# Softmax denominators added up by GpSimd's accumulating transfers instead of VectorE, in an attention and local-attention kernel on one core

## The chip, the cores and the metric

The kernel runs on one core of a Trainium2 chip, in one launch. The metric is the device time of that launch in microseconds (us), the median of several runs. TensorE (PE), VectorE (DVE), ScalarE (ACT), GpSimd (POOL) and the queue of SyncE (SP) run side by side. Each executes its own instructions in the order in which the program gives them, and they wait for one another by semaphores.

## The reference, cut to what matters

`x` is 4 images of 64 x 64 pixels with 256 channels, in float32. Layer 0 is full self-attention over the 4096 pixels of an image; layer 1 is a depthwise 3x3 convolution, two 1x1 convolutions with a GELU between them, and a 3x3 windowed attention. Only layer 0's softmax is touched here.

```python
q = x @ Wq + bq                      # (4, 4096, 32)
k = x @ Wk + bk                      # (4, 4096, 32)
v = x @ Wv + bv                      # (4, 4096, 256)
attn = softmax(einsum('bnd,bmd->bnm', q, k), axis=-1)
x = gamma * einsum('bnm,bmc->bnc', attn, v) + x
# layer 1
h_new = x + up2(gelu(up1(depthwise3x3(x))))
out = h_new + local_attention_3x3(h_new)
```

The softmax is computed as `exp(energy)`, its product with `v`, and a division by the sum of the exponentials, the denominator. This document is about how the denominator is summed.

## The kernel before

The 4 x 4096 queries are cut into 32 slots of 512 queries, 8 slots to an image. A slot goes over the image's 4096 keys in 8 groups `G` of 512 keys, and each group in two halves of 256 keys. So a slot has 16 points, one for each half group; here p(n) with n = 2G + half is the tile of exponentials of point n, 128 x 1024 values (512 KB). The loop `for point in range(points)` writes the order of all the work by hand; no scheduler moves anything. At each point it emits, in this order:

- at the first half of a group: the loads for groups further on (`load_keys`, tile `ka`, `load_values`, tile `v`, both on SP's queue), and `energy`, four matmuls (L333) into the single PSUM tile `e`, one group ahead of the products;
- `weight`, the exponential of one half of `e` into `p` (L341, ACT), two points ahead of the products. The tag `p` has 3 buffers, so p(n+3) overwrites p(n);
- the point's `jobs`: layer 1 of the slots 2 to 5 blocks back (convolution on VectorE, `hidden_part`, `update_part`, `guide_part`, `scores`, `local_product`, `border` and so on). At point 12 stands `local_sum`, a chain on GpSimd of a memset, six additions (L1012) and one or two more (L1015) into `lsum`. At point 14 stands `border`, which ends in one or two small GpSimd operations on `pad` (L910, L914);
- `product(slot, G, half)`, the matmuls of p(n) with `v` into the two banks `acc` (L352);
- `add_up` of p(n+1) into the denominator tile `den`, on VectorE: a copy for p(0) (L363) and an addition for each of p(1) to p(15) (L366). The last call also folds `den` from 1024 to 512 columns (L368);
- steps of the convolution (L505, VectorE), by a fixed table `share`.

After the last point, `partial_sums` transposes `den` and, from slot 4 on, the `lsum` of a slot further back (L386), and reduces both into `parts` (L387). `finish(slot)` then puts a small matmul `dps` (L405) into TensorE's order, straight behind the last product and ahead of the next slot's first `energy`. VectorE takes its reciprocal (L408), spreads it (L394, L397), and scales `acc` into `o` (L417), which frees the `acc` banks for the next slot's first product.

At the start, `project_qk(0)` makes the first queries and keys, and 12 small transfers (L273) on SP's queue copy them into `qa_0` and `ka_0`, where the first `energy` reads them. `fetch(4)` and `fetch(5)` read the pixels of blocks 4 and 5 from HBM (L237), each block in two transfers of 256 KB, one for each half of the channels. GpSimd's queue loads layer 1's weights (`blqk`, `wperc`, `wup1`, `wup2` and others, L80) and computes mixed weights `wmix` from them (L551); they stand in slot 0 at point 8 of GpSimd's order, behind nothing but the setup.

From the second image on, `project_v` makes the values of the next image, through tiles `vs` (2 buffers), which ACT's queue stores to HBM (`packed_v`).

Of the kernel before, what the change touches and what calls it, by code (L numbers as in the profile page):

```python
# [12 lines left out]
ALU = mybir.AluOpType  # L13
# [3 lines left out]
P = 128  # L17
B, H, W, C = 4, 64, 64, 256
# [4 lines left out]
NB = 512  # L23
# [4 lines left out]
TPB = NB // P  # L28
# [25 lines left out]
def attention_then_perception_kernel(  # L54
# [19 lines left out]
    nc = tc.nc  # L74
# [17 lines left out]
    def unshifted():  # L92
# [6 lines left out]
        def tile_of(shape, tag, name, bufs=1):  # L99
            return pool.tile(shape, F32, tag=tag, name=name, bufs=bufs)  # L100
# [19 lines left out]
        def ring(slot):  # L120

            return 1 + slot % RING * RB
# [15 lines left out]
        for r in range(4):  # L138
            nc.scalar.dma_start(
                out=bqk2[r * CQK : (r + 1) * CQK, :], in_=b_qk[:, r % 2 : r % 2 + 1]  # L140
# [17 lines left out]
        for r in range(KR):  # L158
            m = near[r * KW : (r + 1) * KW]
            for half in range(2):  # L160

                for sign in (1, -1):
                    nc.gpsimd.affine_select(
                        out=m[:, half], in_=m[:, half], compare_op=ALU.is_ge, fill=0.0,
# [13 lines left out]
        for q in range(0, P, SQ):  # L178
            part = fold[q : q + SQ].rearrange("p (j r) -> p j r", r=SQ)
            nc.gpsimd.affine_select(  # L180
                out=part, in_=part, compare_op=ALU.not_equal, fill=1.0,
# [15 lines left out]
            return watched[:, i : i + 1]  # L197


        queries, keys, values, staged = {}, {}, {}, {}  # L200

# [10 lines left out]
        def fetch(s):  # L214

            b, g = divmod(s, NBLK)
            if 2 <= s < NBLK:

                if s == 2:
                    both = tile_of([P, NHC, NB], "hid", "xc_2_3")  # L220
                    staged[2], staged[3] = both[:, :CH], both[:, CH:]
                elif s == NBLK - 1:
                    t = tile_of([P, CH, UP + RB, W], "lq", f"xc_{s}")
                    staged[s] = t[:, :, UP:, :].rearrange("p c h w -> p c (h w)")
                elif s > 3:
                    t = tile_of([P, CH, 2, HALO + RB, KW], "h", f"xc_{s}", 3)
                    staged[s] = t.rearrange("p c a h w -> p (c a h w)")[:, : CH * NB].rearrange(
                        "p (c n) -> p c n", c=CH
                    )
            else:  # L230
                staged[s] = tile_of([P, CH, NB], "xc", f"xc_{s}", 2)
            rows = x[b].rearrange("p c (h w) -> p c h w", w=WP)
            at, of = (slice(r, r + RB) for r in (1 + g * RB, ring(s)))
            for c in range(CH):
                to = staged[s][:, c, :].rearrange("p (h w) -> p h w", w=W)
                if s >= RING:
                    nc.sync.dma_start(out=to, in_=rows[:, c, at, 1 : 1 + W])  # L237
                elif c == 0:
                    nc.vector.tensor_copy(to, xv[:, c, of, 1 : 1 + W])
                else:  # L240
                    nc.scalar.copy(to, xv[:, c, of, 1 : 1 + W])
# [50 lines left out]
        def project_v(s, pair, tag="m"):  # L292
            xc = staged[s]
            if s >= NBLK:
                v = tile_of([P, 2, C], "vs", f"vs_{s}_{pair}", 2)
            else:
                if pair == 0:
                    values[0, s] = tile_of([P, TPB, C], "v", f"v_0_{s}", 3)
                v = values[0, s][:, 2 * pair : 2 * pair + 2, :]
            ps = bank(tag, f"v_{s}_{pair}")  # L300
            for i in range(2):
                for kin in range(CH):
                    nc.tensor.matmul(  # L303
                        ps[:, i * C : (i + 1) * C],
                        lhsT=xc[:, kin, bass.ts(2 * pair + i, P)], rhs=wv[:, kin, :],
                        start=(kin == 0), stop=(kin == CH - 1),
                    )
            nc.scalar.copy(v, ps.rearrange("p (t c) -> p t c", c=C))
            nc.scalar.dma_start(
                out=packed_v[:, bass.ts(2 * s + pair, 2 * C)], in_=v.rearrange("p t c -> p (t c)")  # L310
            )
# [11 lines left out]
        energies, weights, sums, accs, lsums, lrdens = {}, {}, {}, {}, {}, {}  # L323
# [34 lines left out]
        def add_up(s, G, half):  # L358

            p = weights[s, G, half]  # L360
            if G == 0 and half == 0:
                sums[s] = tile_of([P, 2, NB], "den", f"den_{s}")
                nc.vector.tensor_copy(sums[s], p)  # L363
                return
            den = sums[s]
            nc.vector.tensor_tensor(den, den, p, ALU.add)  # L366
            if G == NG - 1 and half == 1:
                nc.vector.tensor_tensor(den[:, 0, :], den[:, 0, :], den[:, 1, :], ALU.add)  # L368

        def squares(t):  # L370
# [7 lines left out]
        def partial_sums(s):  # L378


            a = shared(s)
            parts_[s] = tile_of([P, 2, NJ], "parts", f"parts_{s}")
            turneds[s] = tile_of([P, CH, NB], "xc", f"turned_{s}", 2)
            todo = [sums[s][:, 0, :]] + ([] if a is None else [lsums.pop(a)])
            for i, t in enumerate(todo):
                nc.vector.transpose(turneds[s][:, i, :], t)  # L386
                nc.vector.tensor_reduce(  # L387
                    parts_[s][:, i, :], squares(turneds[s][:, i, :]), axis=AX.X, op=ALU.add
                )
            watch(parts_[s][:, : len(todo), :].rearrange("p i j -> p (i j)"))  # L390
# [8 lines left out]
        def finish(s, parts=((0, RB),)):  # L399

            acc = accs.pop(s)
            n = NJ * (1 if shared(s) is None else 2)
            ps = bank("m", f"dps_{s}")[:, :n]
            given = parts_.pop(s).rearrange("p i j -> p (i j)")[:, :n]
            nc.tensor.matmul(ps, lhsT=fold, rhs=given, start=True, stop=True)  # L405
            inverse = tile_of([P, 2, NJ], "inverse", f"inverse_{s}")
            inverses[s] = inverse
            nc.vector.reciprocal(inverse.rearrange("p i j -> p (i j)")[:, :n], ps)  # L408

            rden = sums.pop(s)[:, 1, :]  # L410
            on_all(inverse[:, 0, :], turneds[s][:, 0, :], rden)
            watch(inverse.rearrange("p i j -> p (i j)")[:, :n])
            os = [tile_of([P, NB], "o", f"o_{s}_{c}", 2) for c in range(CH)]
            for r0, r1 in parts:
                n = slice(r0 * W, r1 * W)
                for c, o in enumerate(os):
                    nc.vector.scalar_tensor_tensor(  # L417
                        o[:, n], acc[c][:, n], gam[:, 0:1], rden[:, n], ALU.mult, ALU.mult,
                        accum_out=seen(),
                    )  # L420
                for c, o in enumerate(os):
                    dst = xv[:, c, ring(s) + r0 : ring(s) + r1, 1 : 1 + W]
                    nc.vector.scalar_tensor_tensor(  # L423
                        dst, o[:, n].rearrange("p (h w) -> p h w", w=W), gbv[:, c : c + 1], dst,
                        ALU.add, ALU.add,
                    )
                if len(parts) > 1:
                    yield
            if s < NSLOT - 1:
                rim(s)  # L430
            yield
# [303 lines left out]
        guides, lvs, near_ws, late, results, totals = [], {}, {}, {}, {}, {}  # L735
# [183 lines left out]
        def local_values(s, t):  # L919
            ps = job_bank(f"lv_{s}_{t}")  # L920
            for half in range(2):
                for kin in range(CH):
                    nc.tensor.matmul(  # L923
                        ps[:, half * C : (half + 1) * C],
                        lhsT=keys_of(s, t, half, kin), rhs=wlv[:, kin, :],
                        start=(kin == 0), stop=(kin == CH - 1),
                    )
            for half in range(2):
                if s < NSLOT - 2:
                    lvs[s, t, half] = tile_of([P, C], "lv", f"lv_{s}_{t}_{half}", 8)  # L930
                else:
                    if not half:
                        late[s, t] = late_tile(f"lv_{s}_{t}")
                    lvs[s, t, half] = late[s, t][:, half * C : (half + 1) * C]
                lv = lvs[s, t, half]
                nc.vector.tensor_tensor(lv, ps[:, half * C : (half + 1) * C], blv, ALU.add)
                if s >= NSLOT - 1:

                    square = tile_of([P, 2, NB], "den", f"lv_{s}_{t}_{half}_2")[:, 0, :C]
                    nc.gpsimd.tensor_tensor(square, lv, lv, ALU.mult)  # L940
                    watch(square)

# [145 lines left out]

        fetch(0)
        fetch(1)  # L1090
        fetch(4)
        project_v(0, 0, "acc")
        project_qk(0)
        project_v(0, 1, "acc")
        fetch(2)
        fetch(3)
        fetch(5)
        for i in range(2):
            project_v(1, i)
# [21 lines left out]
        for slot in range(NSLOT):  # L1121
# [3 lines left out]
            k, a = slot - LAG_HID, slot - LAG_ATT  # L1125
# [50 lines left out]
            for point in range(points):  # L1176
                G, half = divmod(point, 2)
# [526 lines left out]
```

## Time and profile before

| what | before |
|---|---|
| median of 3 runs | 3395.23 us (3394.91 to 3396.22) |
| the profiled execution: its own time | 3395.35 us |
| its span, first to last instruction | 3393.6 us |
| PE busy | 3364.7 us (99%) |
| DVE busy | 2747.1 us (81%) |
| ACT busy | 1074.8 us (32%) |
| POOL busy | 352.1 us (10%) |
| granted TensorE clock, mean | 0.998 |
| GpSimd's own transfers (software_dynamic) | 576 packets, 2.53 MB |
| bytes moved by all transfers | 285.17 MB, mean 84 GB/s |

The span is 1.75 us shorter than the execution's own time. A busy PE is one with a matmul under way; matmuls are pipelined, and their ends are modelled. In the lists of groups, the numbers behind the bars are the total busy time and the mean duration in ns of one instruction, then the idle time of that engine just before the group and what ended most of it. In the lists of waits, the numbers are the total, how many times, and the longest. In the timeline, a row has the start, the duration, the engine, the line and operation, output and inputs, a count, and in brackets the idle time before it. In the list of transfers, the last number is the time in us from issue to landing, where the trace can tell it.

### The profile page before, as it was taken

How to read it: one execution, taken by the hardware profiler on the slowest of the kernel's cores; microseconds unless marked ns; L12 is line 12 of the kernel's file. 1: busy time of each engine (PE TensorE's matmuls, PEld its weight loads, DVE VectorE, ACT ScalarE, POOL GpSimd, SP SyncE). 2: the span in 40 equal slices, each digit the busy share in tenths (PEclk: the TensorE clock that was granted, in tenths of full speed). 3: DMA queues.
4: the chain of work that ended last, by engine and by line, in shares of the span. 5: the costliest groups of instructions: out<-in, count | busy, mean ns of one | idle time of the engine just before them, and what ended most of it. 6: DMA issues, size and time to landing. Idle time of an engine off the chain costs nothing.

```text
span 3393.6 us, 32830 instructions
## 1 busy us (share of the span) xinstructions
PE 3364.7 (99%) x11678; PEld 2118.8 (62%) x11678; DVE 2747.1 (81%) x4455; ACT 1074.8 (32%) x1344; POOL 352.1 (10%) x550
## 2 busy tenths in 40 slices
PE   8999999999999999999999999999999999999998
PEld 5556666666666666666666666666666666666655
DVE  2388888867888888876888888887688888988895
ACT  2233333333332333332333323333333333333331
POOL 3000011100111110110001111101110011110031
PEclk9999999999999999999999999999999999999999
DMA  5332222342222222234222222223422222222200
GB/s 170 104 104 65 73 77 78 97 133 89 77 77 81 82 75 71 77 102 140 77 78 78 75 82 83 67 79 107 141 80 68 78 77 70 87 84 66 71 13 26
DMA packets 166126, 285.17 MB, mean 84 GB/s; under 512 B 67284, under 2 KB 68196, under 8 KB 165828
## 3 DMA queue, kind: packets, MB, share of 16 engines
q1 hardware_dynamic: 155684, 263.36, 25.1%
q10 hardware_dynamic: 9696, 17.11, 1.3%
q0 software_dynamic: 576, 2.53, 0.2%
q8 instruction: 95, 1.56, 0.2%
q14 instruction: 75, 0.61, 0.1%
HBM read 240.23 MB, written 41.94 MB: 83 GB/s over the span
## 4 chain that ended last, share of the span: by engine, by line
PE 90%; DVE 7%; DMA 2%; SPq 0%; issue 0%; ACT 0%; ACTq 0%; DVEq 0%; POOL 0%
PE acc L352 47%; PE e L333 7%; PE hid_bc L610 5%; PE hid_de L610 4%; PE hid_gf L610 4%; PE lv L923 3%; DVE perc L505 3%; PE lo L1057 3%; PE v L303 2%; PE hid_a L610 2%; DMA ka<-packed 2%; PE s L964 2%; PE dx_cd L562 1%; PE dx_ab L562 1%; PE dx_eg L562 1%; DVE den L366 1%
## 5 line engine op out<-in xcount | busy, mean ns | idle before, releaser
L352 PE MATMUL acc<-p,v 128*128 128x512 f32 x4096 | 1833.3, 593 | 0.6 <-DVE o L417 0.6
L352 PEld LDWEIGHTS acc<-p,v 128*128 128x128 f32 x4096 | 770.4, 190 | 794.7 <-issue 775.4
L505 DVE SCALAR_TENSOR_TENSOR perc<-xp,wperc,perc 128x512 f32<-128x512 f32 (+2 forms) x1554 | 1108.1, 775 | 27.6 <-ACT perc L501 27.5
L341 ACT ACTIVATE p<-e 128x1024 f32<-128x1024 f32 x512 | 524.8, 1025 | 1676.9 <-PE e L333 758.3
L366 DVE TENSOR_TENSOR den<-den,p 128x1024 f32<-128x1024 f32 x480 | 585.3, 1219 | 74.0 <-ACT p L341 72.2
L333 PE MATMUL e<-qa,ka 128*128 128x512 f32 x1024 | 364.9, 478 | 14.9 <-DMA ka<-packed 8.1
L989 POOL TENSOR_TENSOR lp<-lp,near 128x396 f32<-128x396 f32 x60 | 89.1, 1486 | 2427.8 <-ACT lp L984 2427.8
L333 PEld LDWEIGHTS e<-qa,ka 128*128 128x128 f32 x1024 | 190.5, 190 | 143.8 <-issue 101.8
L610 PE MATMUL hid_de<-perc,wmix 128*128 128x256 f32 x720 | 165.2, 379 | 0.0
L610 PEld LDWEIGHTS hid_de<-perc,wmix 128*128 128x128 f32 x720 | 136.8, 190 | 43.7 <-issue 21.5
L511 DVE TENSOR_TENSOR perc<-perc 128x256 f32<-128x256 f32 x360 | 149.9, 430 | 8.2
L633 ACT ACTIVATE hid<-hid,bup 128x512 f32<-128x512 f32 x120 | 80.4, 717 | 220.0 <-DVE hid L617 220.0
L501 ACT ACTIVATE perc<-xp,bperc,wperc 128x512 f32<-128x512 f32 x192 | 145.9, 809 | 1.7 <-DVE xp L423 1.7
L1012 POOL TENSOR_TENSOR lsum<-lsum,lp 128x99 f32<-128x99 f32 (+1 forms) x179 | 123.7, 698 | 11.7
L923 PE MATMUL lv<-wlv,h 128*128 128x256 f32 x520 | 122.4, 379 | 0.0
L303 PE MATMUL v<-wv,xc 128*128 128x256 f32 x512 | 117.9, 383 | 0.6 <-DMA wv<-in_w_v 0.5
L303 PEld LDWEIGHTS v<-wv,xc 128*128 128x128 f32 x512 | 98.1, 192 | 28.7 <-issue 15.4
L1057 PEld LDWEIGHTS lo<-lp,lv 128*128 128x128 f32 x732 | 104.9, 191 | 17.5 <-issue 9.8
L923 PEld LDWEIGHTS lv<-wlv,h 128*128 128x128 f32 x520 | 98.7, 190 | 15.5 <-issue 2.2
L1057 PE MATMUL lo<-lp,lv 128*128 128x99 f32 (+1 forms) x732 | 104.7, 291 | 0.0
L617 DVE TENSOR_TENSOR hid<-hid_bc,hid 128x512 f32<-128x512 f32 x60 | 41.5, 692 | 75.4 <-PE hid_bc L610 75.4
L341 ACT ACT_TABLE_LOAD x60 | 77.0, 1283 | 76.2 <-PE e L333 75.0
(205 smaller groups left out, 3128.6 us busy)
## 6 DMA issues: line engine op xcount, KB each, us to landing
v<-packed_v SPq DMA_DIRECT2D x248, 512.0 KB
ka<-packed SPq DMA_DIRECT2D x508, 128.0 KB
xp<-in_x SPq DMA_DIRECT2D x30, 528.0 KB
xc<-in_x SPq DMA_DIRECT2D x56, 256.0 KB
out<-lo SPq DMA_DIRECT2D x56, 256.0 KB
packed_v<-vs ACTq DMA_DIRECT2D x48, 256.0 KB
packed<-st SPq DMA_DIRECT2D x16, 512.0 KB
qa<-packed SPq DMA_DIRECT2D x62, 128.0 KB
```

Of the source, the lines that this page charges most:

```text
L303: nc.tensor.matmul(ps[:, i * C : (i + 1) * C], lhsT=xc[:, kin, bass.ts(2 * pair + i, P)], rhs=wv[:, kin, :], start=(kin == 0), stop=(kin = ...
L333: nc.tensor.matmul(e[:, j, :], lhsT=key[:, bass.ts(j, P)].bitcast(F32R), rhs=queries[s].bitcast(F32R), start=True, stop=True,)
L341: nc.scalar.activation(p, energies[s, G][:, 2 * half : 2 * half + 2, :], AF.Exp)
L352: nc.tensor.matmul(accs[s][c], lhsT=v[:, 2 * half + i, bass.ts(c, P)], rhs=p[:, i, :], start=(first and i == 0), stop=(G == NG - 1 and hal ...
L366: nc.vector.tensor_tensor(den, den, p, ALU.add)
L501: nc.scalar.activation(acc, win, AF.Identity, bias=bperc[:, half, j : j + 1], scale=wt)
L505: nc.vector.scalar_tensor_tensor(acc, win, wt, acc, ALU.mult, ALU.add)
L511: nc.vector.tensor_tensor(t[:, to, :], t[:, a, :], t[:, b, :], op)
L610: nc.tensor.matmul(ps[:, n * C : (n + 1) * C], lhsT=w(j), rhs=mixes[s, j][:, kind, :], start=(j == 0), stop=(j == MULT - 1),)
L923: nc.tensor.matmul(ps[:, half * C : (half + 1) * C], lhsT=keys_of(s, t, half, kin), rhs=wlv[:, kin, :], start=(kin == 0), stop=(kin == CH ...
L1012: nc.gpsimd.tensor_tensor(to, to, near_ws[block, half][:, t_, of, :], ALU.add)
L1057: nc.tensor.matmul(pv[:, rows, columns(half)], lhsT=lvs[block, t, half][:, bass.ts(c, P)], rhs=near_ws[block, half][:, t, of, :], start=(i ...
```

## The change

Each slot has two denominator tiles, one for the first halves and one for the second halves of the groups, each with 2 buffers. At group 0 VectorE copies p(0) and p(1) into them. For p(2) to p(15), 14 half groups, GpSimd issues a transfer from `p` to the tile of its half with `accum_op=ALU.add`: the transfer adds what it reads to what is there. Each such transfer waits for the one before it on the same tile. At the end of the slot VectorE adds the two tiles, and folds the sum as before.

The space for the second tile comes from `vs`, which goes: the values of the next image's blocks now go through the tag `late` (3 buffers of a whole block). At the start, `fetch(4)` moves from ahead of `project_v(0)` and `project_qk(0)` to behind `fetch(3)`, and so behind the 12 transfers of L273 on SP's queue.

In the order of GpSimd's instructions of the changed program, from slot 4 on, the accumulation of p(13) stands behind `local_sum`, then comes that of p(14), then `border`'s operations on `pad`, then the accumulation of p(15), which waits for that of p(13). In slot 0 the weight transfers and the mixing stand between the accumulations of p(9) and p(10).

```diff
@@ project_v
             if s >= NBLK:
-                v = tile_of([P, 2, C], "vs", f"vs_{s}_{pair}", 2)
+                if pair == 0:
+                    fresh[s] = tile_of([P, TPB, C], "late", f"vs_{s}", 3)
+                v = fresh[s][:, 2 * pair : 2 * pair + 2, :]
@@ add_up
             p = weights[s, G, half]
-            if G == 0 and half == 0:
-                sums[s] = tile_of([P, 2, NB], "den", f"den_{s}")
-                nc.vector.tensor_copy(sums[s], p)
+            if G == 0:
+                sums[s, half] = tile_of([P, 2, NB], "den", f"den_{s}_{half}", 2)
+                nc.vector.tensor_copy(sums[s, half], p)
                 return
-            den = sums[s]
-            nc.vector.tensor_tensor(den, den, p, ALU.add)
+            nc.gpsimd.dma_start(out=sums[s, half], in_=p, accum_op=ALU.add)
             if G == NG - 1 and half == 1:
+                den, other = (sums[s, i] for i in range(2))
+                nc.vector.tensor_tensor(den, den, other, ALU.add)
                 nc.vector.tensor_tensor(den[:, 0, :], den[:, 0, :], den[:, 1, :], ALU.add)
@@ partial_sums
-            todo = [sums[s][:, 0, :]] + ([] if a is None else [lsums.pop(a)])
+            todo = [sums[s, 0][:, 0, :]] + ([] if a is None else [lsums.pop(a)])
@@ finish
-            rden = sums.pop(s)[:, 1, :]
+            rden = sums.pop((s, 0))[:, 1, :]
@@ the start
         fetch(0)
         fetch(1)
-        fetch(4)
         project_v(0, 0, "acc")
         project_qk(0)
         project_v(0, 1, "acc")
         fetch(2)
         fetch(3)
+        fetch(4)
         fetch(5)
```

The other edits rename the keys of `sums` and give the tile of the squares in the last slots the same two buffers.

More of the change, by code (lines that the diff above doesn't have):

```diff
@@ L197, in seen @@
             return watched[:, i : i + 1]
-        queries, keys, values, staged = {}, {}, {}, {}
+        queries, keys, values, fresh, staged = {}, {}, {}, {}, {}
         packed = tc.dram_tile([NSLOT // 2, 2, 2, 2, CQK, NB], F32, name="packed")
@@ L937, in local_values @@
                 if s >= NSLOT - 1:
-                    square = tile_of([P, 2, NB], "den", f"lv_{s}_{t}_{half}_2")[:, 0, :C]
+                    square = tile_of([P, 2, NB], "den", f"lv_{s}_{t}_{half}_2", 2)[:, 0, :C]
                     nc.gpsimd.tensor_tensor(square, lv, lv, ALU.mult)
```

## The prediction

> **What bounds the kernel now.** I read the page first, then who waits for whom on TensorE, then the end of one slot (slot 10, 977 to 1077 us) engine by engine. The page's first part and its group of the removed additions:
>
> ```profile
> PE 3364.7 (99%) x11678; PEld 2118.8 (62%) x11678; DVE 2747.1 (81%) x4455; ACT 1074.8 (32%) x1344; POOL 352.1 (10%) x550
> ...
> L366 DVE TENSOR_TENSOR den<-den,p 128x1024 f32<-128x1024 f32 x480 | 585.3, 1219 | 74.0 <-ACT p L341 72.2
> ```
>
> TensorE is idle for 3393.6 - 3364.7 = 28.9 us in all. Its waits:
>
> ```profile
> PE e L333 <- DMA ka<-packed: 8.1, 9, 2.3
> PE e L333 <- DMA packed_v<-v: 6.7, 1, 6.7
> PE dps L405 <- DVE parts L387: 1.2, 6, 0.2
> ...
> PE g L811 <- DVE h L673: 1.0, 1, 1.0
> PE c L907 <- DVE edge L896: 0.7, 3, 0.2
> PE acc L352 <- DVE o L417: 0.6, 1, 0.6
> ```
>
> VectorE, busy as it is, costs TensorE 1.2 + 1.0 + 0.7 + 0.6 = 3.5 us. Making it faster buys next to nothing; making any operand of TensorE later costs its full lateness. So the question is where the denominator is due. The timeline at the end of slot 10, VectorE and then TensorE:
>
> ```profile
> 1071.85 1.22 DVE L366 TENSOR_TENSOR den<-den,p 128x1024 f32<-128x1024 f32 x1
> ...
> 1075.98 0.69 DVE L387 TENSOR_REDUCE parts<-turned 128x16 f32<-128x512 f32 x1
> ```
>
> ```profile
> 1069.48 7.13 PE L352 MATMUL acc<-p,v 128*128 128x512 f32 x16
> 1076.82 0.38 PE L405 MATMUL dps<-parts,fold 128*128 128x32 f32 x2 [0.20 <-DVE parts L387]
> ```
>
> From the last addition to the end of `parts` is 1076.67 - 1071.85 = 4.82 us, and `dps` starts 0.15 us later, already 0.20 us late. The denominator has no slack at a slot's end. GpSimd in the same stretch:
>
> ```profile
> 1063.75 4.55 POOL L1012 TENSOR_TENSOR lsum<-lsum,lp 128x99 f32<-128x99 f32 x6
> 1068.38 0.24 POOL L1015 TENSOR_TENSOR lsum<-lsum,pad 1x16 f32<-1x16 f32 x1
> 1070.49 0.45 POOL L910 TENSOR_SCALAR pad<-pad 1x80 f32<-1x80 f32 x1 [1.88 <-ACT pad L909]
> 1071.02 0.21 POOL L914 TENSOR_SCALAR pad<-pad 1x2 f32<-1x2 f32 x1
> ```
>
> **The change part by part.** VectorE loses 480 - 32 = 448 additions of 1.219 us, 546 us, and gains 32 copies (L363) of 0.69 us, 22 us. None of the 524 us lies on TensorE's path but the 3.5 us above.
>
> The new path is this. In slot 10 `local_sum` holds GpSimd until 1068.62. Only then is the accumulation of p(13) issued. Let L be the time from issue to landing. That of p(15) must wait for the landing of p(13), at 1068.62 + L, and for the `pad` operations, done at 1071.23; for L over 2.6 us the first is later. It lands at 1068.62 + 2L. Then VectorE's 4.82 us follow (one addition of the same size, the fold, two transposes, two reductions), so `parts` ends at 1073.44 + 2L instead of 1076.67: **2L - 3.2 us more wait of TensorE per slot**. Behind `dps` in TensorE's order stands the whole next slot, so nothing hides it. VectorE's blocked addition has only its own chain and `finish` behind it. The exponentials of the next slot's p(0), which overwrites p(13), move from 1069.17 to 1068.62 + L or later, and p(1) waits for p(14), which lands at most one transfer later; their reader stands behind `dps` as well and finds them ready.
>
> No accumulating transfer is in the trace. GpSimd's plain ones are, in the list of transfers:
>
> ```profile
> wup<-in_w_up POOLq DMA_DIRECT2D x1, 1536.0 KB, 9.1
> ...
> wperc<-in_w_perc POOLq DMA_DIRECT2D x1, 27.0 KB, 2.8
> ...
> bperc<-in_b_perc POOLq DMA_DIRECT2D x1, 3.0 KB, 2.7
> ```
>
> A small one takes 2.7 us, the fixed part. 1536 KB take 6.4 us more, so 512 KB take 2.1 us; at the highest rate that the windows show, 351 GB/s (18 to 24 us), 1.5 us. An accumulation must read its target as well as its source, so twice that. The lower end is L = 2.7 + 1.5 = 4.2 us (once, fast), the upper 2.7 + 2 x 2.1 = 7.0 us. I take 2.7 + 2 x 1.5 = 5.7 us, since source and target are both in SBUF and the high rate was for a mix of transfers. Then 2L - 3.2 = 8.2 us.
>
> The Trainium skill (DMA: Bandwidth & Descriptors, Anatomy of one DMA) puts a GpSimd transfer at 2.0 us plus bytes over 436 GB/s; by that estimate L is 3.2 us, 2L - 3.2 is 3.2 us, and the 24 slots below cost 77 us instead of 197. The page on collectives (Collectives: The Full Stack, Why ReduceScatter is half of AllGather) speaks against the change: adding in flight reads two sources and halves the rate; no row here shows it yet.
>
> 24 slots (4 to 30 without 7, 15 and 23) have this shape: 24 x 8.2 = 197 us. Slots 7, 15 and 23 carry projections at points 14 and 15, some 4 us more cover: 3 x 4 = 12. Slots 0 to 3 have no `local_sum`, and p(15) is exponentiated 10 us before the last product's end: 0.
>
> **TensorE's clock.** After a wait the windows show half clock for a while (columns: stretch, length, busy of PE, PEld, DVE, ACT, POOL, clock, DMA share, GB/s):
>
> ```profile
> 18.00:24.00 6.00, 0.00 (x0) 0.01 (x1) 0.69 (x1) 0.61 (x2) 0.00 (x0) 0.83 0.94 351
> 24.00:28.50 4.50, 4.48 (x11) 3.59 (x12) 0.00 (x0) 1.94 (x2) 4.14 (x3) 0.50 1.11 325
> ```
>
> There four `energy` matmuls took 2.05 us against 1.17 us in slot 10, and 16 of `project_v` 5.05 us against 3.62 at 49.96 us: 2.3 us lost after a wait of 6.7. After the wait of 2.3 us that ends at 55.9 us I count 1.7 (four `energy` 1.90 against 1.17, four products 2.82 against 1.88). The wait of 1.5 us near 42 us left the clock whole. So each wait of over 2.3 us costs about 2 more: 27 x 2 = 54 us.
>
> **Two crowded transfer engines.** While only `ka` is moving, the windows show this:
>
> ```profile
> 980.00:985.00 5.00, 5.00 (x21) 3.77 (x20) 3.42 (x8) 1.10 (x2) 0.00 (x0) 1.00 0.14 52
> ```
>
> 0.14 of 16 engines is two engines, for 5 us in every group, since 52 GB/s x 5 us is the two 128 KB pieces. `v` takes 1.5 us more. The two accumulations of a group add 2 x 3 us on every engine: 12.5 us per group on those two. A steady slot has (100 + 8 + 2)/8 = 13.8 us per group, enough. Slots 1 and 2 last 66 us, 8.3 us per group, so up to 8 x 4.2 = 34 us each; loads issued two groups ahead give some back, and I take 25 each, 50 us. At 1.5 us per accumulation this would be 10 each; at 4.2 us (15 per group) the steady slots would become bound too, by some 7 us each.
>
> **Slot 0.** GpSimd's weight loads and mixing now stand between p(9) and p(10). Before, they took from 16.1 to 38.8 us, beside the setup. p(10)'s buffer is due three points later, some 16 us, with p(13) needed two points after that: 0 to 9 us, I take 5.
>
> **The start.** The 6.7 us wait ended with the small L273 transfers, at a DMA share of 0.94: `fetch(4)` was ahead of them on SP's queue, and the 1536 KB of `wup1` beside them. Both now go later. At most 6.7 us and the 2.3 us of half clock go, 9; at least 0; I take 6. Next late there is the `qk` chain itself. Blocks 4 and 5 are needed at 38.6 us, and have 15 us from their new issue. The `late` tile for `vs` only adds buffers: 0.
>
> **Sum.** 197 + 12 + 54 + 50 + 5 - 6 = 312 us. The profiled execution took 3395.35 us (span 3393.6, 1.75 us around it; 0.1 us from the median), so 3707 us.
>
> **The rivals.** (A) The relief pays and the wait stays hidden: TensorE gains 3.5 us, up to 9 at the start and some 2 in the tail, 3383 us. It decides at the slot's end: p(15)'s transfer would have to land by 1071.9, an L under 0.7 us behind `pad`, and no row of this queue is under 2.7. Chance 0.03. (B) Transfers as quick as the smallest row, L = 2.7 to 3.8: a wait of 2.2 to 4.4 us in 24 slots, 53 to 106 us, little or half of the clock's 54, no crowding: 3440 to 3530 us, say 3490. For it speaks that nothing but two SBUF ends is touched; against it that 27 KB alone take 2.8. Chance 0.12. (C) My forecast, L from 3.8 to 7: 3530 to 4000 us. Chance 0.65. (D) Adding in flight is several times slower than copying, and the transfer engines bound the kernel: at 5.5 us each, a group needs 17.5 us on the two engines, 140 per slot, 4200 us or more; the trace has nothing for or against it. Chance 0.19. (E) That the adds do not move is excluded by the changed program's order of instructions; 0.01 for no change from some other cause.
>
> **How the numbers follow.** 3707 us is case C. The low end, 3530, is L = 4.2: 24 x 5.2 + 3 = 128, clock 27, less 9, 146 us, and a little of B. The high end, 4000, is L = 7.0 (24 x 10.8 = 259, 20, clock 70), crowding of the steady slots (27 x 7 = 189) and 70 in slots 0 to 2, 608 us. A measurement can tell about 0.2%, 7 us: faster by more 0.03, within it 0.01, slower by more 0.96.
>
> **What would show it.** Right: a new wait of TensorE at `dps` for `parts`, some 27 times of 4 to 11 us; behind it VectorE's addition (now L370) waiting for transfers; a clock of 0.5 in places at each slot's start; `ka` waits in slots 1 and 2; GpSimd's transfers at a share near 36% (448 x 3 us of 3707); VectorE's busy time near 2220 us; the first `energy` before 20 us. Wrong: `dps` without a wait (then A), TensorE waiting mostly on `ka` in steady slots (then D), or on `p` through its three buffers, which I priced at nothing.

## The result, and the profile after

The changed kernel takes 3979.14 us (median of 4 runs, 3965.83 to 3992.36); beside it the kernel before took 3395.07 us. The ratio is 1.1721, 95% interval 1.1701 to 1.1741. The profiled execution took 3982.85 us, with a span of 3981.1 us, 587.5 us more than before. The page of the changed kernel: busy times, GpSimd's queue, and the groups of the new path.

```profile
PE 3498.5 (88%) x11678; PEld 2197.4 (55%) x11678; DVE 2218.1 (56%) x4039; ACT 1073.4 (27%) x1344; POOL 784.4 (20%) x998
...
q0 software_dynamic: 65088, 237.44, 31.6%
...
L370 DVE TENSOR_TENSOR den<-den,den 128x1024 f32<-128x1024 f32 x32 | 39.2, 1225 | 766.8 <-DMA den<-p 766.8
...
den<-p POOLq DMA_DIRECT2D x448, 512.0 KB, 7.8
```

VectorE lost 529 us of work, where 524 were forecast, and the kernel is 584 us slower all the same. An accumulation takes 7.8 us from issue to landing (the median of 448). TensorE's waits in the changed kernel:

```profile
PE dps L408 <- DVE parts L390: 316.2, 30, 14.1
PE e L335 <- DMA ka<-packed: 137.9, 44, 10.7
PE e L335 <- ACT p L343: 14.1, 8, 2.9
...
PE e L335 <- DMA ka<-st: 0.4, 1, 0.4
```

This accounts for the whole span. TensorE's idle time grew from 28.9 to 482.6 us, which is 453.7; `dps` and `ka` make 438 of it. Its busy time grew from 3364.7 to 3498.5, which is 133.8, with the same number of matmuls: the record of the granted clock shows one half for 485 us, in 57 stretches (before: 18 us, in 3). Together 587.5 us.

The end of slot 10 in the changed kernel, the timelines of GpSimd, ScalarE, VectorE and TensorE; the last product ends at 1281.58:

```profile
1271.83 1.78 POOL L367 DMA_DIRECT2D den<-p  x2
...
1281.02 0.41 POOL L913 TENSOR_SCALAR pad<-pad 1x80 f32<-1x80 f32 x1 [7.40 <-ACT pad L912]
...
1281.73 0.87 POOL L367 DMA_DIRECT2D den<-p  x1
```

```profile
1279.71 1.02 ACT L343 ACTIVATE p<-e 128x1024 f32<-128x1024 f32 x1 [6.71 <-DMA den<-p]
1280.63 0.30 ACT L912 ACTIVATE pad<-c,small 1x80 f32<-1x80 f32 x1
```

```profile
1289.60 1.22 DVE L370 TENSOR_TENSOR den<-den,den 128x1024 f32<-128x1024 f32 x1 [22.99 <-DMA den<-p]
```

```profile
1294.57 0.60 PE L408 MATMUL dps<-parts,fold 128*128 128x32 f32 x2 [12.98 <-DVE parts L390]
1294.98 2.05 PE L335 MATMUL e<-qa,ka 128*128 128x512 f32 x4
```

Read it downwards. p(13) and p(14) are issued together when `local_sum` ends, at 1271.83 and 1272.41. p(13) lands 7.77 us later, at 1279.60. At 1279.71 ScalarE, which had waited 6.71 us for this landing, writes the next slot's p(0) over p(13). Behind that stands `border`'s `pad`, then GpSimd's two `pad` operations, and only then is p(15) issued, 2.13 us after p(13) has landed. It lands 7.77 us later still, and VectorE starts 0.10 us after that. `dps` comes 12.98 us late, and the four `energy` matmuls behind it take 2.05 us, the half clock.

### The profile page after: what moved, and what is told of

Read it like the earlier page. It is cut to its first block, busy times and chain, and to the rows that moved or that the text cites. A ratio compares the mean times of both kernels' runs of the same rounds, so it can differ in the third digit from the quotient of the medians.

```text
span 3981.1 us, 33220 instructions
## 1 busy us (share of the span) xinstructions
PE 3498.5 (88%) x11678; PEld 2197.4 (55%) x11678; DVE 2218.1 (56%) x4039; ACT 1073.4 (27%) x1344; POOL 784.4 (20%) x998
## 3 DMA queue, kind: packets, MB, share of 16 engines
q0 software_dynamic: 65088, 237.44, 31.6%
## 4 chain that ended last, share of the span: by engine, by line
PE 63%; DMA 19%; POOL 6%; DVE 6%; issue 3%; SPq 2%; ACT 1%; DVEq 0%; ACTq 0%; POOLq 0%
PE acc L354 28%; DMA den<-p 11%; DMA ka<-packed 8%; PE e L335 5%; PE hid_bc L613 4%; PE hid_de L613 4%; PE hid_gf L613 4%; POOL lp L992 4%; PE hid_a L613 3%; PE lv L926 3%; PE lo L1060 2%; DVE perc L508 2%; POOL lsum L1015 2%; SPq L212 1%; PE dx_ab L565 1%
## 5 line engine op out<-in xcount | busy, mean ns | idle before, releaser
L508 DVE SCALAR_TENSOR_TENSOR perc<-xp,wperc,perc 128x512 f32<-128x512 f32 (+2 forms) x1554 | 1049.5, 741 | 81.0 <-ACT perc L504 81.0
L367 POOL DMA_DIRECT2D den<-p x448 | 387.1, 880 | 1977.5 <-ACT p L343 1106.8
L335 PE MATMUL e<-qa,ka 128*128 128x512 f32 x1024 | 391.6, 510 | 155.7 <-DMA ka<-packed 137.9
L370 DVE TENSOR_TENSOR den<-den,den 128x1024 f32<-128x1024 f32 x32 | 39.2, 1225 | 766.8 <-DMA den<-p 766.8
L335 PEld LDWEIGHTS e<-qa,ka 128*128 128x128 f32 x1024 | 210.0, 215 | 305.9 <-issue 241.1
L408 PE MATMUL dps<-parts,fold 128*128 128x32 f32 (+1 forms) x64 | 17.7, 367 | 316.2 <-DVE parts L390 316.2
L992 POOL TENSOR_TENSOR lp<-lp,near 128x396 f32<-128x396 f32 x60 | 205.1, 3419 | 449.5 <-ACT lp L987 445.7
L613 PE MATMUL hid_a<-perc,wup 128*128 128x256 f32 x360 | 119.2, 482 | 0.0
L967 PEld LDWEIGHTS s<-lq,h 128*128 128x128 f32 x520 | 106.0, 218 | 19.5 <-issue 7.7
```

The costliest lines, as they stand in the source:

```text
L335: nc.tensor.matmul(e[:, j, :], lhsT=key[:, bass.ts(j, P)].bitcast(F32R), rhs=queries[s].bitcast(F32R), start=True, stop=True,)
L367: nc.gpsimd.dma_start(out=sums[s, half], in_=p, accum_op=ALU.add)
L508: nc.vector.scalar_tensor_tensor(acc, win, wt, acc, ALU.mult, ALU.add)
L613: nc.tensor.matmul(ps[:, n * C : (n + 1) * C], lhsT=w(j), rhs=mixes[s, j][:, kind, :], start=(j == 0), stop=(j == MULT - 1),)
L992: nc.gpsimd.tensor_tensor(pv, pv, mask, ALU.mult)
```

## The experiments

The runs were made in groups of four (1 to 4, 5 to 8, 9 to 12), each group on one chip beside the kernel before, which took 3394.53, 3395.80 and 3394.28 us (medians) there.

**Run 1: `ka` on 16 engines.**

```diff
@@ load_parts
-            for i in range(2):
-                of = part[i : i + 1].to_broadcast([2, CQK, NB]) if which else part
-                nc.sync.dma_start(out=to[2 * i * CQK : 2 * (i + 1) * CQK, :], in_=of)
+            for i in range(4):
+                of = part[i // 2] if which else part[i % 2]
+                nc.sync.dma_start(out=to[i * CQK : (i + 1) * CQK, :], in_=of)
```

> The changed kernel, with each ka and qa load cut into four transfers of 32 partitions (16 engines each) instead of two of 64 (one engine each). Theory 1 (an accumulation takes long because two of the 16 engines are also moving ka): the time from issue to landing falls from the median of 7.8 us to about 5 at all positions, the wait of dps from 13 us to about 2 x 5 - 3.2 = 7 us in 24 slots, the ka waits from 138 us to under 30, the half clock from 134 us to about 90: 3640 to 3720 us. Rival (adding in flight takes 8 us by itself): dps stays near 316 us, only the ka waits go, 3820 to 3900 us.

Measured: 3794.70 us (ratio 1.1178, 1.1159 to 1.1196), between the two ranges. TensorE's waits in this run:

```profile
PE dps L408 <- DVE parts L390: 321.3, 29, 14.2
PE e L335 <- ACT p L343: 8.1, 6, 5.6
PE e L335 <- DMA ka<-packed: 7.7, 2, 5.8
```

The two crowded engines cost 187 us of the span: 130 in waits for `ka` and 54 in half clock, the rest in small waits. (The expectation has each old load on one engine. SP's 4-byte packets grow from 8484 to 25584 with this edit, by 17100; if each engine ends its part of a load with one of them, that is 1140 loads on 16 engines less 570 on two.) The median from issue to landing does fall, to 5.2 us, and that of p(11) and p(12) to 4.6 and 4.5, but at the end of a steady slot p(13), p(14) and p(15) still take 7.0, 10.3 and 6.9 us (medians; 7.8, 10.8 and 7.8 without this edit). What p(13) and p(15) gain is lost again: without the waits for `ka`, p(13) is issued only 8.1 us ahead of the last product's end instead of 9.7. So the wait of `dps` stays as it was.

**Run 2: p(12) to p(15) on VectorE again.**

```diff
@@ add_up
-            nc.gpsimd.dma_start(out=sums[s, half], in_=p, accum_op=ALU.add)
+            if 2 * G + half < 12:
+                nc.gpsimd.dma_start(out=sums[s, half], in_=p, accum_op=ALU.add)
+            else:
+                nc.vector.tensor_tensor(sums[s, half], sums[s, half], p, ALU.add)
```

> The changed kernel, with p(12) to p(15) added by VectorE again; p(2) to p(11) stay on GpSimd's queue. Theory 1 (the last two accumulations, behind local_sum, make the wait of dps): the wait of dps falls from 316 us to under 15, the ka waits stay near 100 to 138 us, the half clock falls from 134 us to under 60: 3520 to 3600 us. Rival (the queue is late as a whole, and VectorE now waits for p(10) and p(11) instead): dps still waits 100 us or more, 3700 us or more.

Measured: 3533.51 us (1.0415, 1.0398 to 1.0433). The first line of TensorE's waits is now this:

```profile
PE e L335 <- DMA ka<-packed: 119.5, 46, 10.4
```

There is no wait at `dps` any more, and the half clock lasts 93 us instead of 485. The 128 additions cost VectorE 159 us and TensorE nothing. The last four transfers of a slot made the wait, not the queue as a whole.

**Run 3: both edits.**

> Both edits of the two runs before together. If the slot's end, the two crowded engines and the half clock behind their waits are the whole loss: 3390 to 3440 us, with under 30 us of ka waits and under 15 of dps. Rival (GpSimd's queue, its slower local_sum or p's three buffers cost something of their own): over 3480 us.

Measured: 3399.16 us (1.0015, 1.0005 to 1.0025). TensorE's waits:

```profile
PE e L335 <- DMA ka<-packed: 9.3, 2, 7.5
PE e L335 <- ACT p L343: 4.5, 1, 4.5
PE dps L411 <- DVE parts L393: 4.2, 6, 0.7
```

Three causes, then, hold 580 of the 584 us, net: the slot's end, the two crowded engines, and the half clock behind both. And 320 accumulations, all but hidden outside the first slot (run 10), with VectorE 340 us less busy than before, buy nothing.

**Run 4: no accumulations.**

```diff
@@ add_up
-            nc.gpsimd.dma_start(out=sums[s, half], in_=p, accum_op=ALU.add)
@@ the start
+        nc.vector.tensor_scalar(gam, gam, 0.0, None, ALU.mult)
```

> The changed kernel without the 14 accumulations per slot (the sum leaves out p(2) to p(15), and gamma is set to zero so that no large value goes on). What is left is VectorE's relief of 524 us, the moved fetch(4) and the buffers. By the prediction's terms the relief is worth up to 3.5 us and the start 6: 3384 to 3390 us. Rival (the start's gain is given back when the second group's ka comes): 3391 to 3396 us. Rival of another sign (the moved fetch(4) makes slot 0 slower by itself): over 3397 us.

Measured: 3389.81 us (0.9989, 0.9979 to 0.9998): VectorE's relief, the moved `fetch(4)` and the new buffers together give 4.7 us. The start has hardly a part in it: the first `energy` stands at 23.69 us, and before at 24.02. TensorE and GpSimd in this run:

```profile
23.69 2.05 PE L335 MATMUL e<-qa,ka 128*128 128x512 f32 x4 [6.28 <-DMA ka<-st]
```

```profile
15.06 0.53 POOL L80 DMA_DIRECT2D wup<-in_w_up  x1
```

`fetch(4)` is out of the way here, and `energy` still waits 6.28 us. In the changed kernel that wait was 0.40 us. What differs is GpSimd's weight load of 1536 KB: here it is issued at 15.06 us, there at 82.38, behind the accumulation of p(9).

**Run 5: `border` first** (on top of run 1).

```diff
@@ the loop over points, at point 14
+                behind = point == points - 2 and slot < NSLOT - 1
-                if after[0] < NSLOT:
+                if after[0] < NSLOT and not behind:
                     weight(*after, half)
                 for do in jobs[point]:
                     do()
+                if behind:
+                    weight(*after, half)
```

> The changed kernel with ka on 16 engines (3794.7 us), and at point 14 the job border is emitted ahead of the exponential of the next slot's p(0). Theory 1 (p(15) is issued 1.58 us after p(13) has landed because ScalarE's exponential into p(13)'s buffer waits for that landing, and border's pad stands behind it on ScalarE, then on GpSimd): p(15) is issued at once when p(13) has landed, the wait of dps falls by 1.6 us in 24 slots, to about 283 us in all: 3750 to 3760 us. Rival (p(15)'s packets stand behind p(14)'s in any case): it is issued earlier and lands when it did, 3785 to 3800 us.

Measured: 3778.53 us, 16 less than run 1 and between the two ranges. p(15) is indeed issued 0.3 us after p(13) has landed instead of 1.6 (medians of the steady slots). Against the last product's end it is issued 1.4 us earlier and lands only 0.5 us earlier, because it takes 7.7 us instead of 6.9. The loop through ScalarE and `pad` exists, and more than half of what its removal gains is given back in the transfer: both theories hold in part.

**Run 6: p(14) alone on VectorE** (on top of run 1).

```diff
@@ add_up
-            nc.gpsimd.dma_start(out=sums[s, half], in_=p, accum_op=ALU.add)
+            if 2 * G + half == 14:
+                nc.vector.tensor_tensor(sums[s, half], sums[s, half], p, ALU.add)
+            else:
+                nc.gpsimd.dma_start(out=sums[s, half], in_=p, accum_op=ALU.add)
```

> The changed kernel with ka on 16 engines, and p(14) alone added by VectorE. Theory 1 (p(14), issued 0.6 us after p(13), shares the engines with it and then stands ahead of p(15), so that the end is a chain of three transfers and not of two): p(13) and p(15) land within about 5 us each instead of 7, the wait of dps falls from 12.8 to about 9 us in 24 slots, 3680 to 3710 us. Rival (the loads of v and xp, which move at the same time, lengthen them): the wait stays over 11.5 us, 3760 us or more.

Measured: 3780.37 us; `dps` still waits some 12.2 us in a steady slot, instead of 12.7. The time is in the rival's range, but half of theory 1 holds: without p(14) ahead of it p(15) lands in 4.5 us instead of 6.9, while p(13) takes 8.6 us instead of 7.0 (medians). Slot 10 of this run, GpSimd and SP's queue:

```profile
1166.19 0.87 POOL L370 DMA_DIRECT2D den<-p  x1
...
1177.13 0.88 POOL L370 DMA_DIRECT2D den<-p  x1
```

```profile
1165.57 0.34 SPq L287 DMA_DIRECT2D v<-packed_v  x1
1166.00 0.55 SPq L127 DMA_DIRECT2D xp<-in_x  x1
1166.61 2.12 SPq L212 DMA_DIRECT2D ka<-packed  x4
```

p(15), at 1177.13, moves its first packet 1.5 us after issue and lands in 4.51 us. p(13), at 1166.19, is issued just behind `v` and `xp`, 1040 KB; its first packet moves 4.3 us after issue, when theirs are nearly through (the last of `xp` starts before 1172), and it lands in 8.80 us. In 17 of the 24 steady slots the load of `v` is issued 0.6 us ahead of p(13), as here.

**Run 7: `local_sum` behind p(13)** (on top of run 1).

```diff
@@ jobs
-                job(scores, k, 1) + job(local_sum, k - 1), job(border_terms, k), job(border, k), [],
+                job(scores, k, 1), job(border_terms, k), job(border, k), [],
@@ behind add_up
+                    if point == 12 and slot < NSLOT - 1:
+                        for do in job(local_sum, k - 1):
+                            do()
```

> The changed kernel with ka on 16 engines, and local_sum emitted behind the accumulation of p(13) instead of ahead of it. Theory 1 (the lateness begins with local_sum holding back p(13)): p(13) is issued 4 us earlier and has landed when p(14) is issued; p(15) follows the pad operations at about 5 us ahead of the last product's end and lands about 6 us later; the wait of dps falls from 12.8 to 5 to 7 us, 3580 to 3640 us. Rival (p(13)'s exponential or its predecessor p(11) holds it as long): under 2 us per slot, over 3740 us.

Measured: 3688.10 us, 107 less than run 1, between the two ranges; `dps` waits 8.3 us in a steady slot instead of 12.7. p(13) is issued 4.6 us earlier and lands 5.8 us after that; the gain is smaller than expected because p(14) and p(15) take 8.2 and 8.6 us, where I had put 6 for p(15). Of the four edits to run 1 that keep these accumulations (5, 6, 7 and 9) it gains most by far: `local_sum` had held p(13) back.

**Run 8: plain copies instead of accumulations.**

```diff
@@ add_up
-            nc.gpsimd.dma_start(out=sums[s, half], in_=p, accum_op=ALU.add)
+            nc.gpsimd.dma_start(out=sums[s, half], in_=p)
@@ the start
+        nc.vector.tensor_scalar(gam, gam, 0.0, None, ALU.mult)
```

> The changed kernel with plain copies in place of the accumulations (the same 448 transfers without the adding; the sum keeps only the last two half groups, and gamma is zero). Two engines carry ka as in the changed kernel. Theory 1 (the adding's second read doubles the packets' time): packets of 4096 bytes 159 to 175 ns instead of 338, the shortest transfers about 3.1 us instead of 4.5, those beside ka about 6.5 instead of 7.8; the ka waits fall from 138 us to under 60, dps from 316 to about 180 to 250: 3700 to 3820 us. Rival (issue, fixed part and waiting in the queue make most of the time, whatever is moved): over 3880 us.

Measured in one run: 3809.16 us, in the range of theory 1.

```profile
PE dps L408 <- DVE parts L390: 210.1, 30, 11.1
PE e L335 <- ACT p L343: 52.6, 25, 3.6
PE e L335 <- DMA ka<-packed: 46.2, 12, 10.8
```

Packets of 4096 bytes take 160 ns instead of 338, the quickest transfers 2.8 us instead of 4.5, the median 6.5 instead of 7.8. The `ka` waits fall from 137.9 to 46.2 us, `dps` from 316.2 to 210.1, while the waits of `energy` for ScalarE's `p` rise from 14.1 to 52.6. So the adding is worth some 170 us here, and mere copies would still cost some 413, from order and traffic.

**Run 9: `xp` later** (on top of run 1).

```diff
@@ the loop over slots
             if slot >= RING:
-                renew(slot)
+                pass
@@ the loop over points
+                if point == 2 and slot >= RING:
+                    renew(slot)
```

> The changed kernel with ka on 16 engines (3794.7 us), and the load of the next rows of xp (528 KB) emitted at point 2 of the slot instead of ahead of point 0. Theory 1 (p(13) and p(15) land late because the loads of v and xp, which start when p(13) does, are ahead of them on the same engines): the first packets of p(13) come about 2 us earlier, dps waits 1.5 to 4 us less in 24 slots: 3690 to 3755 us. Rival (the adding is slow there for another reason): 3780 to 3800 us.

Measured: 3792.43 us, no difference. The edit did not separate the theories. `xp` is issued 8.6 us behind p(13) instead of 0.5 (slot 10), still ahead of the slot that it is emitted in, so it only moved from beside p(13) and p(14) to beside p(15). In slot 10, p(14) then takes 9.0 us instead of 10.5, p(15) 8.3 instead of 7.1, and p(13), beside `v` and `ka`, 7.0 as before: 1.2 to 1.5 us go to whichever accumulation meets `xp`. How much of p(13)'s 7 us is due to `v` and how much to `ka` was not tried.

**Runs 10 to 12: is there a version that beats both?** Run 10 is run 3 with only p(2) and p(3) accumulated in slot 0. Runs 11 and 12 are the kernel before with `load_parts` of run 1, `fetch(4)` moved as in the change, and one accumulation in the whole kernel, at `n` = 2 or 9, which keeps GpSimd's weight loads waiting behind it:

```diff
@@ add_up of the kernel before
-            nc.vector.tensor_tensor(den, den, p, ALU.add)
+            if s == 0 and 2 * G + half == n:
+                nc.gpsimd.dma_start(out=den, in_=p, accum_op=ALU.add)
+            else:
+                nc.vector.tensor_tensor(den, den, p, ALU.add)
```

> As the run with both edits (3399.2 us: ka on 16 engines, p(12) to p(15) on VectorE), but in slot 0 only p(2) and p(3) go by accumulation. Theory 1 (GpSimd's weight loads and mixing in the middle of slot 0's accumulations cost that kernel some 10 us there, and behind p(3) they are still late enough to leave the first energy alone): slot 0 falls from 104 to about 95 us, 3386 to 3392 us. Rival (the weights' 3 MB, now moving at 35 us, delay the second and third ka as much): 3395 to 3402 us.

Measured: 3398.68 us (1.0014, 1.0005 to 1.0023), in the rival's range, and only in part for its reason. Slot 0, from its first product to the next slot's, falls from 104.3 to 99.4 us; the weights, now moving from 35 us on, leave the `ka` of group 3 (counted from 0, the "third" of the expectations) 9.1 us late, where it was 7.5. The 4.9 us go again at the program's end: an instruction DRAIN of GpSimd's (L1705) lasts 6.72 us instead of 0.89, and the span ends 10.0 us after VectorE's last operation instead of 5.3, though the last store landed 6.8 us before that end. Why it lasts longer was not tried.

> The kernel before, with ka on 16 engines, fetch(4) moved as in the change, and one single accumulation, that of slot 0's p(2), which holds GpSimd's weight loads back until 32 us. Theory 1 (the 6.7 us wait at the start is made by the weight loads on GpSimd's queue and not by fetch(4); ka on two engines makes the 8 us of ka waits): the first energy at about 17.7 us, 3380 to 3389 us. Rival (the loads come back as ka waits later in slot 0): 3390 to 3396 us.

Measured: 3387.33 us (0.9978, 0.9969 to 0.9987). The time is in the range of theory 1, but half of the rival is true as well. The first `energy` is at 17.07 us, and the `ka` of group 3 is again late:

```profile
52.09 2.05 PE L333 MATMUL e<-qa,ka 128*128 128x512 f32 x4 [7.80 <-DMA ka<-packed]
```

> As the run before this one, with the single accumulation at slot 0's p(9), which holds the weight loads back until some 75 us. Theory 1: the first energy at 17.7 us, and no weight load beside slot 0's second and third ka: 3378 to 3386 us. Rival (the second and third ka are late because the values and keys of the first image have just been stored, whatever GpSimd does): 3386 to 3394 us, and the same as the run before.

Measured: 3376.95 us (0.9948, 0.9934 to 0.9961), 17 us faster than the kernel before, 1 us under the range of theory 1, and the fastest here. With the weights issued at 65 us, the same `energy` waits for nothing:

```profile
44.23 1.28 PE L333 MATMUL e<-qa,ka 128*128 128x512 f32 x4
```

Its span is 18.4 us shorter than before: 9.2 until the first product starts, 4.0 in slot 0, 5.1 in slots 7, 15 and 23, where `ka` is no longer late. What the move of `fetch(4)` adds beside the held weights was not run by itself.

## Why the prediction was right, and where its terms were not

The direction, the bound and the mechanism were right; the sizes were not. The forecast was 3707 us and the result 3979, near the upper end of the range: a loss of 584 us where the sum had 312. The range held it because its upper end added a slow L and crowded steady slots; the first came and was passed, the second came in part (81 us for 189). (By its own figures the crowding there is 8 x 1.2 = 9.6 us per slot and not 7.) Term by term, on the profiled execution (the waits measured are whole ones; before had 9.3 us of them for `ka` and `dps`):

| term | predicted | measured |
|---|---|---|
| `dps`, 24 steady slots | 197 | 296.9 |
| `dps`, slots 7, 15, 23 | 12 | 11.5 |
| `dps`, slots 0 to 3 | 0 | 7.8 |
| `energy` waits, slots 1 and 2 | 50 | 43.4 |
| `energy` waits, slot 0 behind the first | 5 | 30.4 |
| `energy` waits, other slots | 0 | 81 |
| half clock | 54 | 133.8 |
| start, first wait | -6 | -6.3 |

**The slot's end was mis-sized by its L.** The step 2L - 3.2 us stands, with L = 7.8 us instead of 5.7, above even the 7.0 that I gave as its upper end: 4.2 us more per slot. I took the doubled packet time and the fixed part, but an empty queue. Alone on the engines the accumulation is even quicker than I took it, 4.5 us. Beside `ka` on two engines it has to wait for those two: 8 packets of 338 ns and 64 of 84 ns are 8.1 us of work on each, and run 1 brings p(11) and p(12) from 7.8 and 8.2 us to 4.6 and 4.5. I had named that load and let it delay only `ka`. At the slot's end this is the smaller part: p(13) and p(15) keep 7.0 and 6.9 us in run 1. There p(13) stands behind the packets of `v` and `xp` (run 6), and p(15) meets p(14) (run 6) or `xp` (run 9).

**A wait that I priced at nothing was in the chain.** The text says that the exponential over p(13) moves and that its reader finds it ready. But ScalarE keeps its order, and `pad` stands behind that exponential, ahead of p(15)'s issue on GpSimd. "The `pad` operations, done at 1071.23" was a time of the old order. It made the chain 2L + 2.1 in slot 10 (2L + 1.6 in the median slot); run 5 removed it. Against that, `local_sum` ended 9.75 us ahead of the last product's end instead of 8.0. In sum for slot 10: 8.2 + 4.2 + 2.1 - 1.7 = 12.8 us, measured 12.98. Slots 7, 15 and 23 came out at 11.5 us for 12 by luck: with L = 7.8 the 4 us of cover that I gave them would have left some 8 us each, and they waited 3.8. What slots 1 to 3 wait, 7.8 us for the 0 I put, was not looked into.

**The steady slots were bound by the two engines at times.** The average, 12.5 us of work in 13.8 us, left no wait; single groups did wait, 2 to 4 us per slot. I kept this case for the upper end of the range only. Run 1 shows it whole: with `ka` on 16 engines these waits go. In slot 0, 13.3 us of waits stay even then, against 3.3 in run 4: 10 us that come with slot 0's accumulations, for the 5 I took; the crowded engines made the rest. Run 10 does not part them further, since it moves the weights as well.

**The clock's price was nearly right, its count was not.** 133.8 us over 57 stretches is 2.3 us each, beside the 2 I took; but there were 57 and not 27, because the `ka` waits bring their own: in run 1, with 7.7 us of them left, there are 33.

**The start was right by number and wrong by cause.** I gave the gain to two moves, `fetch(4)` and the weights. Run 4 has only the first, and the wait is still there. Of the gain, 6.1 us were lost again two groups on: the `energy` of group 2 waited 7.6 us for `ka` where it had waited 1.5. That is the two engines once more, since in run 1 it waits 1.9.

**VectorE's relief** is worth about the 3.5 us claimed: 4.7 us in run 4, the buffers and the start with it. VectorE's busy time (2218 for 2220), the first `energy` (17.6 us) and the share of GpSimd's transfers (31.6%, for 36% at the forecast's 3707 us) came as listed.

The two pages, against the runs. The Trainium skill (DMA: Bandwidth & Descriptors, Anatomy of one DMA) gives 3.2 us for 512 KB by that estimate; plain copies with nothing beside them took 2.8 to 2.9 us in run 8, so the rule comes near for what it describes; an accumulation in traffic took 2.4 times that estimate. The page on collectives (Collectives: The Full Stack, Why ReduceScatter is half of AllGather) says of ReduceScatter that adding in flight reads two sources and halves the rate: 338 ns per packet against 160 in run 8 agrees.

## What to carry to other kernels

Before an addition is moved from an engine to transfers, look for the due time of its last result and for everything else that moves at that moment: a transfer that takes 4.5 us on idle engines took 7.8 exactly where it was due, and the late waits were charged again by the clock, 133.8 us in all. An engine that is 81% busy and makes the bound engine wait 3.5 us in all is not worth relieving. Spread broadcast loads over all transfer engines, and hold bulk loads that nobody needs yet behind something late: together, with `fetch(4)` moved, that was worth 17 us here.

## What the runs showed of the hardware that was not expected

- The `ka` load, whose outer dimension is 2, keeps two transfer engines busy (a share of 0.14 of 16 while it moves alone), and an accumulation spread over all of them lands late beside it: p(11) and p(12) took 7.8 and 8.2 us, and 4.6 and 4.5 with that load cut into four (run 1).
- Weight loads on GpSimd's queue (1536 and 512 KB, issued at 15 and 16 us) made small transfers of SP's queue, issued from 11 us on, some 6 us late: TensorE waited 6.28 us for them in run 4, and 0.40 in the changed kernel, which issues the weights at 82 us.
- GpSimd's additions in `scores` (128 x 396) took 1.49 us before, 3.42 in the changed kernel, 3.41 in run 4, which has no accumulations, and 1.39 in run 3. In the changed kernel 28 of the 60 take some 6.2 us, beside convolution steps on VectorE (L508). They are quick in all kernels whose VectorE still adds p(12) to p(15), and slow in all others; why was not tried, and in run 4 it costs TensorE nothing that shows.
- The DRAIN of GpSimd's that ends the program lasts 0.8 to 0.9 us in kernels with 9, 10 and 329 transfers on GpSimd's queue, 2.7 with 457, 6.7 with 321 (run 10) and 6.6 with 425 (run 6). This was not expected and not tried further.
